# The last attention loop by blocks of queries with its own closing beside it, choice and gathering by image, and smaller groups of work in the fill

## The chip, the core and the metric

The kernel runs on one core of a Trainium2 chip. The core has a tensor engine (PE, with PEld for its loads of weights), a vector engine (DVE), a scalar engine (ACT), GpSimd (POOL) and SyncE (SP); each takes its instructions in order, and each of SP, ACT and POOL also issues DMAs from its own queue. The metric is the device time of one execution in microseconds, as the median of three runs.

## The reference, cut to what matters

There are two layers on x of four images, 4096 tokens (64 by 64) and 128 channels. Names are shortened here.

```python
# layer 0: three selective scans (forward, backward, sliced) over the tokens
xz = in_proj(groupnorm(x))                       # 256 channels u and 256 channels z, per token
for d in (forward, backward, sliced):            # d is an order of the tokens
    u = silu(causal_conv1d(u_d, conv_w, conv_b))           # 4 taps
    dt_raw, B, C = x_proj(u)                               # 8, 16 and 16 rows
    delta = softplus(dt_w @ dt_raw + dt_b)
    h[t] = h[t-1] * exp(delta[t] * A) + delta[t] * u[t] * B[t]   # 256 channels x 16 states
    y_d = (sum over states of h * C + D * u) * silu(z)
x = x + out_proj(y_f + y_b + y_s)

# layer 1, attention: 16 heads of width 8, q = k = v
t = layernorm(x)
q = ring_of_cosines(t + theta)
ctx = softmax(q q^T / sqrt(8)) q                 # 4096 x 4096 per head and image
x1 = layernorm(t + ctx @ w_comb.T + b_comb)
zf = cos(x1[:, :8]) * cos(ry)
t = x + layernorm(x1 + relu(zf @ w1.T + b1) @ w2.T + b2)

# layer 1, experts: 64 experts, each takes its 8 best tokens of an image
xn = layernorm(t)
probs = softmax(xn @ gate_w.T + gate_b, axis=tokens)
vals, idx = top_k(probs, 8)                      # per image and expert
pooled = sum over the 8 of xn[idx] * vals        # 64 x 128 per image
out = gelu(pooled @ weight1) @ weight2           # with bias rows
t = t + scatter_add(idx, out * vals)             # on the tokens that were chosen
```

All data are 32-bit floats.

## The kernel before, in words

**Order.** The program is recorded by hand: generators give one step at a `yield`, and a `Pace` turns credits into steps (`run(0.5)` gives half a step, so one step in two calls). Each engine then runs its instructions in the order in which they were recorded. `flow(pieces, width, apart)` runs up to `width` generators in turn, and starts the next one when the last one started has made `apart` steps. `Bank` hands out banks of PSUM; a piece that finds none yields and tries again.

**The fill** (up to about 2447 us). `Inputs` makes the inputs of the scans for all four images: per image `norm`, then for each of three orders four chunks of 1024 tokens (`of_chunk`), and beside the third order the four pieces of `gate`. A chunk is a convolution on PE (tile `cv`), Silu on ACT, projections on PE (`xd`, `dt`), a softplus in pieces (Abs and Relu, Exp, Ln and two Identity passes on ACT; three matmuls per half that sum them in tile `sp`, L415), an addition on DVE (L417), a product on DVE (L421) and stores to DRAM by POOL. Beside it `Scans.of_image(0)` runs the 384 scan steps of image 0. A step loads spread rows of delta and du, takes exp on ACT (L496), and has three instructions on DVE: product (L505), scan (L508), product (L510). Every four steps PE sums over the states in tile `y` (L516), and DVE adds D times u in tile `o` (L532), which POOL stores. The two are interleaved one step of scan to 0.98 steps of inputs. A matrix A for each order is loaded by 96 small DMAs on the ACT and POOL queues; `scan_weights` then takes its exp on ACT (L198) in the same place, before ACT copies the first normed tokens (L274).

**The opening and loops 0 to 2** (up to about 10453 us). After a short stage for the first `opening`, an attention `loop` runs per image, with the scans of the next image, the `opening` of the next and the closing (`after`) of the one before beside it. A loop has 1024 rounds: 4 groups of heads j, 8 blocks of 512 queries qb, 32 blocks of 128 keys kc, nested in this order. A round has eight passes for scores (L846), two exponentials of 128x1024 on ACT (L851, so 2048 per loop) and eight passes for sums over keys (L860). At the last kc, ACT copies the accumulator (tile `av`, L869), and POOL stores it: four DMAs to `d_ctx` (L875) and one to `d_sum` (L878).

**Closing.** `after(b)` inverts the sums of the softmax (`shares`: load of `sum`, L922, store of `d_share`), then for eight blocks of 512 tokens: `first` (loads of x, `cT` and `part`, product L937, `co` matmuls L944, normalization) and, after one cosine for all, `second` (`zt` L965, `h` L978, `fo` L988, two normalizations, `xT` L1009, `lg` L1017, stores to `d_t`, `d_xn` and `d_lg`). The loop has one bank of PSUM for all of it.

**Loop 3** (from about 10453 to 12813 us) has `after(2)`, `biases` and `gather(0)` beside it, at half a step per round. `gather(j)` takes two images at once: `choice` (Max8 over 4096 logits L1088, Exp with sums L1095, Max8 again L1101, match_replace L1105, a product L1107, a product with the share L1109) and eight `pool` calls (transposes `wt` L1124, matmuls `pool` L1133).

**The end** (12813 us on). `after(3)` in five parallel pieces with seven banks, `gather(1)`, then `answers`: 16 groups of four experts (`h` L1169, `hT`, Gelu L1187, `o` L1192), whose weights come as `w1` on the SP queue (1 MB per group) and four `w2` DMAs on the ACT queue (1 MB in all). Two groups of weights are recorded before the closing, three after `gather(1)`. At last `scatter` adds the answers to the tokens (L1253, L1260) and stores `out`.

Of the kernel before, what the change touches and what calls it, by code (L numbers as in the profile page):

```python
# [16 lines left out]
P = 128  # L17
C = 128
# [116 lines left out]
def scan_weights(nc, const, load, load_ps, ident, in_proj_w, out_proj_w, dirs):  # L135
# [55 lines left out]
    for i, (d, w) in enumerate(zip(dirs, ws)):  # L191
# [6 lines left out]
        nc.scalar.activation(w["A"], w["A"], AF.Exp)  # L198
        nc.vector.tensor_scalar_mul(w["A"], w["A"], -1.0)
# [3 lines left out]
class Inputs:  # L203
# [29 lines left out]
    def bank(self, name):  # L233
        while self.held == 3:
            yield
        self.held += 1
        return self.ps.tile([P, T], F32, tag="a", name=name)
# [17 lines left out]
    def norm(self, b):  # L255

        nc = self.nc
        while b - 1 in self.gated and self.gated[b - 1] < NC:
            yield
# [54 lines left out]
    def gate(self, b, g):  # L314
        nc, xn = self.nc, self.normed[b]
        s_g = self.piece.tile([P, 2, T], F32, tag="u", bufs=2, name=f"z_{b}_{g}")
        for m in range(2):
# [7 lines left out]
            yield  # L325
            nc.scalar.activation(s_g[:, m, :], ps, AF.Silu)
# [5 lines left out]
    def of_chunk(self, b, order, c):  # L332
        while b not in self.normed or (order == 2 and b not in self.sliced):
            yield
# [23 lines left out]
        for m in range(2):  # L358
            ps = yield from self.bank(f"cv_{key}_{m}")
            for g, cut in enumerate(halves):  # L360
                for k in range(4):
                    nc.tensor.matmul(  # L362
                        ps[:, cut], w["conv"][:, k, m * P : (m + 1) * P], reads(k, g), start=(k == 0), stop=(k == 3)
                    )
            banks.append(ps)
            yield
# [17 lines left out]
        while self.middle:  # L384
            yield
# [20 lines left out]
        nc.scalar.activation(ln, e, AF.Ln, bias=1.0)  # L406
# [3 lines left out]
        yield  # L410
        for m in range(2):
# [4 lines left out]
            yield  # L416
            nc.vector.tensor_add(r[:, m, :], r[:, m, :], ps)  # L417
# [9 lines left out]
class Scans:  # L427
# [23 lines left out]
    def of_image(self, b, made, queue=None):  # L451
# [18 lines left out]
        def load(s):  # L470
# [7 lines left out]
            for name, bufs in (("delta", 3), ("du", 4)):  # L478
                t = self.deep.tile([P, T], F32, tag=name, bufs=bufs, name=f"{name}_{b}_{s}")
                src = made[b, order, c][name][at : at + 16]  # L480
                by = queue if queue is not None and name == "du" else nc.sync
# [74 lines left out]
        for s in range(self.AHEAD):  # L556
            yield from have(s)
            load(s)
        exp(0)
# [8 lines left out]

        for s in range(n):
            if s + self.AHEAD < n:  # L570
                yield from have(s + self.AHEAD)
            late = s >= 4 and s % 4 in (1, 2)
            if late and s % 4 == 1:
# [9 lines left out]
            if late:  # L583
# [4 lines left out]
            if late and s % 4 == 2:  # L588
                out(s - 3, y)
                self.bank.leave()  # L590
            yield
            self.steps[b] += 1
        while not self.bank.free:
# [6 lines left out]
        out(n - 1, y)  # L600
        self.bank.leave()
# [3 lines left out]
class Attention:  # L605
# [3 lines left out]
    def __init__(self, tc, ctx, w, gate, cols, ident, bank, dram, t1, w_out, sums, sz, x):  # L609
# [63 lines left out]
        self.xn, self.logits, self.angled = {}, {}, {}  # L673
# [146 lines left out]
    def loop(self, b, beside):  # L820
# [3 lines left out]
        self.total[b] = self.dram.tile([H, L], F32, name=f"d_sum_{b}")  # L824
# [5 lines left out]
        rounds = [(j, qb, kc) for j in range(4) for qb in range(L // QB) for kc in range(NT)]  # L830
# [35 lines left out]
        def sums(j, qb, i):  # L866
# [5 lines left out]
            def store():  # L872
                for k in range(4):
# [5 lines left out]
                    out=self.total[b].rearrange("(k j) t -> j k t", j=4)[j, :, cut], in_=av[D::32, :]  # L879
                )  # L880

# [15 lines left out]
        for i in sorted(later):  # L897
            later[i]()

    def after(self, b):  # L900

        nc = self.nc
        tiles = self.t1[b].rearrange("(t p) c -> p t c", p=P)
        mid = self.dram.tile([P, NT, C], F32, name=f"d_x1_{b}")
        share = self.dram.tile([H, L], F32, name=f"d_share_{b}")
        self.t2[b] = self.dram.tile([P, NT, C], F32, name=f"d_t2_{b}")
        self.xn[b] = self.dram.tile([P, NT, C], F32, name=f"d_xn_{b}")
        if b // 2 not in self.logits:
            self.logits[b // 2] = self.dram.tile([2, E, L], F32, name=f"d_lg_{b // 2}")
        z = self.small.tile([P, NT, D], F32, tag="z", bufs=1, name=f"z_{b}")  # L910
# [7 lines left out]
        def shares():  # L918
            t = self.piece([P, 512], "p0", name=f"sum_{b}")
            nc.sync.dma_start(out=t, in_=self.total[b].rearrange("h (c t) -> (h c) t", t=512))  # L920
            yield
            nc.vector.reciprocal(t, t)  # L922
            nc.gpsimd.dma_start(out=share.rearrange("h (c t) -> (h c) t", t=512), in_=t)
            yield

        def first(g):
# [7 lines left out]
                out=part, in_=share[:, g * 512 : (g + 1) * 512].unsqueeze(1).to_broadcast([H, D, 512])  # L934
# [22 lines left out]
        def second(g):  # L957
# [14 lines left out]
            while self.hidden == self.n - 1:  # L972
                yield
            self.hidden += 1
            h = self.one.tile([P, 4, 512], F32, tag="h", bufs=self.n - 1, name=f"h_{b}_{g}")
# [46 lines left out]
            nc.gpsimd.dma_start(out=self.logits[b // 2][b % 2, :, g * 512 : (g + 1) * 512], in_=lg)  # L1022
# [394 lines left out]
```

## Time and profile before

| | us |
|---|---|
| median of 3 runs | 13271.63 (13271.44 to 13279.25) |
| the profiled execution, its time | 13276.74 |
| its span, first to last instruction | 13275.0 |
| last product of the fill's inputs (L421) starts | 2438.2 |
| first exponential of loop 3 | 10456.1 |
| last exponential of loop 3 | 12812.2 |
| busy over the span: PE, DVE, ACT, POOL | 12311.7, 8963.1, 10702.1, 3471.0 |

The page gives the busy time of every engine over the span, and the span in 40 equal slices of 332 us with a digit for each engine. Slices 1 to 8 are the fill, 9 to 31 the loops 0 to 2, 32 to 38 loop 3, and the last one and a half the end. A table of stretches gives the busy time of each engine in each stretch with the granted clock of PE and the DMA load. In groups by line, the last part of a row says how long the engine was idle ahead of these instructions, and what ended the idle time. The chain of waits follows the work that ended last back from the end.

### The profile page before, as it was taken

To read this page: it belongs to the slowest core of one execution; us is meant where nothing else is said; L and a number is where in the kernel's file an instruction comes from. 1 tells how busy PE (TensorE), PEld (TensorE's weight loads), DVE (VectorE), ACT (ScalarE), POOL (GpSimd) and SP (SyncE) were. 2 spreads that over 40 slices of the span, in tenths; PEclk is the share of its full clock that TensorE was granted. 3 is DMA by queue.
4 is the path that set the end of the run, shared out by engine and by line. 5 is a ranking of instruction groups with operands and counts; after the bars stand their busy time and mean duration, and the time that the engine had idled before them with its cause. 6 is when DMAs were issued, how large, how long until landed. Compare 5 with 4: busy or idle time off the path is not lost. (4 is left out here: it accounts for less than half of the span.)

```text
span 13275.0 us, 213812 instructions
## 1 busy us (share of the span) xinstructions
PE 12311.7 (93%) x85255; PEld 3959.8 (30%) x85255; DVE 8963.1 (68%) x8565; ACT 10702.1 (81%) x10807; POOL 3471.0 (26%) x4198
## 2 busy tenths in 40 slices
PE   7797879489999999999999999999999999999976
PEld 3333333222222222233332222333222222222224
DVE  6998989788888876988888778888874110000014
ACT  5665756289999998999999989999998888888851
POOL 2333334222333332333333223333331000000001
PEclk9888888699999999999999999999999999999986
DMA  5666666544444445544444454444443100000015
GB/s 143 185 185 176 190 175 195 172 127 118 121 121 117 115 119 136 130 109 117 114 106 114 116 140 126 110 114 114 112 107 96 43 16 9 9 18 21 12 36 180
DMA packets 686881, 1482.04 MB, mean 112 GB/s; under 512 B 184894, under 2 KB 301942, under 8 KB 685878
## 3 DMA queue, kind: packets, MB, share of 16 engines
q1 hardware_dynamic: 495182, 1049.44, 30.7%
q0 software_dynamic: 139584, 300.84, 7.3%
q10 hardware_dynamic: 51112, 118.08, 3.3%
q8 instruction: 667, 10.93, 0.3%
q14 instruction: 336, 2.75, 0.1%
HBM read 1158.83 MB, written 308.94 MB: 111 GB/s over the span
## 5 line engine op out<-in xcount | busy, mean ns | idle before, releaser
L851 ACT ACTIVATE e<-s 128x1024 f32<-128x1024 f32 x8192 | 7904.5, 1027 | 1015.6 <-PE s L846 788.9
L846 PE MATMUL s<-qm,qT 32*128 32x512 f32 x32768 | 5416.4, 642 | 109.4 <-DMA qT<-d_q 58.8
L860 PE MATMUL acc<-e,v 128*32 128x512 f32 x32768 | 4387.0, 607 | 23.0 <-ACT av L869 20.0
L509 POOL COPY ends<-h 128x1 f32<-128x1 f32 x1536 | 1835.7, 1195 | 4934.0 <-DVE h L508 4920.3
L846 PEld LDWEIGHTS s<-qm,qT 32*128 32x128 f32 x32768 | 1789.8, 184 | 3266.4 <-issue 1453.6
L860 PEld LDWEIGHTS acc<-e,v 128*32 128x32 f32 x32768 | 647.6, 108 | 3158.2 <-issue 3019.3
L508 DVE TENSOR_TENSOR_SCAN h<-dA,ends,dB 128x1024 f32<-128x1024 f32 x576 | 1374.4, 2386 | 186.1 <-ACT dA L496 128.0
L508 DVE TENSOR_TENSOR_SCAN h<-delta,ends,du 128x1024 f32<-128x1024 f32 x576 | 1354.1, 2351 | 160.0 <-ACT delta L496 88.5
L505 DVE TENSOR_TENSOR dB<-du,B 128x1024 f32<-128x1024 f32 x768 | 935.3, 1218 | 204.3 <-PE y L516 185.8
L496 ACT ACTIVATE dA<-delta,A 128x1024 f32<-128x1024 f32 x768 | 887.9, 1156 | 213.5 <-DMA delta<-d_delta 152.2
L496 ACT ACTIVATE delta<-delta,A 128x1024 f32<-128x1024 f32 x768 | 887.3, 1155 | 180.7 <-PE y L516 170.2
L510 DVE TENSOR_TENSOR du<-h,C 128x1024 f32<-128x1024 f32 x768 | 940.7, 1225 | 26.3
L510 DVE TENSOR_TENSOR dB<-h,C 128x1024 f32<-128x1024 f32 x768 | 940.7, 1225 | 26.3
L505 DVE TENSOR_TENSOR du<-du,B 128x1024 f32<-128x1024 f32 x768 | 933.9, 1216 | 0.0
L875 POOL DMA_DIRECT2D d_ctx<-av x512 | 262.6, 521 | 1646.4 <-ACT av L869 1642.8
L362 PE MATMUL cv<-xn,conv 128*128 128x512 f32 x1024 | 492.2, 640 | 40.6 <-DVE xn L299 26.5
L516 PE MATMUL y<-dB,sel 128*32 128x256 f32 x6144 | 496.0, 396 | 16.4 <-DVE o L532 16.4
L516 PE MATMUL y<-du,sel 128*32 128x256 f32 x6144 | 492.0, 393 | 6.1 <-DVE du L510 6.1
L508 DVE TENSOR_TENSOR_SCAN h<-dA,dB 128x1024 f32<-128x1024 f32 x192 | 446.9, 2328 | 56.8 <-ACT dA L496 35.4
L532 DVE SCALAR_TENSOR_TENSOR o<-us,D,y 128x256 f32<-128x256 f32 x384 | 206.2, 537 | 412.1 <-PE y L516 398.6
L508 DVE TENSOR_TENSOR_SCAN h<-delta,du 128x1024 f32<-128x1024 f32 x192 | 440.1, 2292 | 38.9 <-ACT delta L496 15.3
L415 PE MATMUL sp<-s,minus 128*128 128x512 f32 x384 | 223.1, 665 | 208.2 <-ACT s L409 208.2
(248 smaller groups left out, 7714.6 us busy)
## 6 DMA issues: line engine op xcount, KB each, us to landing
delta<-d_delta SPq DMA_DIRECT2D x768, 512.0 KB
du<-d_du SPq DMA_DIRECT2D x576, 512.0 KB
du<-d_du ACTq DMA_DIRECT2D x192, 512.0 KB
d_u<-u POOLq DMA_DIRECT2D x48, 1024.0 KB, 5.7
B<-d_bc SPq DMA_DIRECT2D x96, 512.0 KB
C<-d_bc SPq DMA_DIRECT2D x96, 512.0 KB
d_delta<-r POOLq DMA_DIRECT2D x48, 1024.0 KB, 5.4
d_du<-u POOLq DMA_DIRECT2D x48, 1024.0 KB, 6.7
```

The lines of the kernel that those rows point to most:

```text
L362: nc.tensor.matmul(ps[:, cut], w["conv"][:, k, m * P : (m + 1) * P], reads(k, g), start=(k == 0), stop=(k == 3))
L415: nc.tensor.matmul(ps[:, cut], sign, t[:, m, cut], start=(i == 0), stop=(i == 2))
L496: nc.scalar.activation(tiles["delta", s], t, AF.Exp, scale=A)
L505: nc.vector.tensor_mul(dB, du, spread[order, c, "B", j % 2])
L508: nc.vector.tensor_tensor_scan(h, dA, dB, first, ALU.mult, ALU.add)
L509: nc.gpsimd.tensor_copy(ends[order, c][:, at : at + 1], h[:, T - 1 :])
L510: nc.vector.tensor_mul(dB, h, spread[order, c, "C", j % 2])
L516: nc.tensor.matmul(y[32 * g : 32 * g + 32, : T // 4], self.sel[:, j // 2, :], hC[:, 256 * g : 256 * g + 256], start=(j == 0), stop=(j == 3),)
L846: nc.tensor.matmul(s_ps[:, k, :], qT[at : at + 32, kc * P : (kc + 1) * P], queries[j, qb][at : at + 32, :], start=True, stop=True,)
L851: nc.scalar.activation(e, s_ps, AF.Exp, scale=1.0 / math.sqrt(D))
L860: nc.tensor.matmul(accs[j, qb][32 * k : 32 * k + 32, :], v[:, kc, h * VW : h * VW + 32], es[i][k // 2][:, k % 2, :], start=(kc == 0), stop ...
L875: nc.gpsimd.dma_start(out=self.context[b][h * D : h * D + D, cut], in_=av[32 * k : 32 * k + D, :])
```

## The change

Five things are changed.

- **Fill.** A yield stands behind every half of a convolution and of a softplus sum; both additions L417 of a chunk come together, one step after the last matmul; Ln is recorded behind the two Identity passes. The two generators are interleaved 1 to 1.5, a second piece starts 10 steps behind the first in place of 6. The scans of image 0 have two banks in place of one, and `finish` (tile `o`) is recorded two scan steps later. The exp of A moves to just ahead of the first exp of the scans.
- **Loop 3 by blocks.** The last loop goes over qb outside and j inside, and `whole` tells when a block of queries has all its heads. `after` takes a range of blocks: 0 to 3 and 4 to 6 of image 3 are recorded beside loop 3, block 7 behind it. The share is 0.92 steps per round, and 1.5 once seven blocks are whole.
- **By image.** Logits are kept per image. `gather` takes images (0, 1), then 2, beside loop 3, and 3 at the end. `search` takes the eight best logits of seven blocks of image 3 ahead; the end looks at these 8 and the 512 of block 7.
- **Choice.** There is one Max8 in place of two (the eight values found go through Exp themselves), and no product with the share: it goes into a diagonal that replaces the identity in `wt` (now matmuls of 64 columns), and into `answers`.
- **End.** Four groups of weights are recorded right behind the loop and a fifth behind the closing; the closing has one piece in flight.

In the order of the changed program the closing of image 2 spans rounds 8 to 420 of loop 3, pool calls of images 0, 1 and 2 rounds 441 to 657, blocks 0 to 3 of image 3 rounds 667 to 870, blocks 4 to 6 rounds 903 to 995, and the search of image 3 follows at round 997. Between the fill and loop 3, the order on every engine is that of before.

```diff
@@ scan_weights
-        nc.scalar.activation(w["A"], w["A"], AF.Exp)
-        nc.vector.tensor_scalar_mul(w["A"], w["A"], -1.0)
@@ Inputs.of_chunk
                     nc.tensor.matmul(
                         ps[:, cut], w["conv"][:, k, m * P : (m + 1) * P], reads(k, g), start=(k == 0), stop=(k == 3)
                     )
+                yield
             banks.append(ps)
-            yield
+        yield
...
         nc.scalar.activation(e, e, AF.Exp, scale=-1.0)
-        nc.scalar.activation(ln, e, AF.Ln, bias=1.0)
         yield
         nc.scalar.activation(s, e, AF.Identity, bias=1.0)
         nc.scalar.activation(s, s, AF.Identity, bias=self.minus_one)
         yield
+        nc.scalar.activation(ln, e, AF.Ln, bias=1.0)
+        yield
+        banks = []
         for m in range(2):
             ps = yield from self.bank(f"sp_{key}_{m}")
             for cut in halves:
                 for i, (sign, t) in enumerate(((self.ident, e), (self.minus, s), (self.ident, ln))):
                     nc.tensor.matmul(ps[:, cut], sign, t[:, m, cut], start=(i == 0), stop=(i == 2))
-            yield
-            nc.vector.tensor_add(r[:, m, :], r[:, m, :], ps)
+                yield
+            banks.append(ps)
+        yield
+        for m in range(2):
+            nc.vector.tensor_add(r[:, m, :], r[:, m, :], banks[m])
             self.leave()
@@ Scans.of_image
+        if b == 0:
+            for w in self.ws:
+                nc.scalar.activation(w["A"], w["A"], AF.Exp)
+                nc.vector.tensor_scalar_mul(w["A"], w["A"], -1.0)
         exp(0)
...
+        def finish(s, y):
+            out(s, y)
+            self.bank.leave()
...
             step(s)
-            if late and s % 4 == 2:
-                out(s - 3, y)
-                self.bank.leave()
+            if turn == 2 and not alone:
+                finish(s - 3, y)
+            if turn == 0 and alone and s >= 8:
+                finish(s - 5, y)
@@ Attention.loop
+        turns = [(j, qb) for j in range(4) for qb in range(L // QB)]
+        if by_block:
+            turns.sort(key=lambda turn: turn[1])
+        rounds = [(j, qb, kc) for j, qb in turns for kc in range(NT)]
...
+                if by_block and j == 3:
+                    self.whole[b] = qb + 1
@@ Attention.after
-    def after(self, b):
+    def after(self, b, gs=range(L // QB)):
...
+        while self.whole[b] < blocks.stop:
+            yield WAIT
...
         yield from shares()
-        yield from flow((first(g) for g in range(NT // 4)), self.n, 8 // self.n)
+        yield from flow((first(g) for g in gs), self.n, 8 // self.n)
         yield from cosines()
-        yield from flow((second(g) for g in range(NT // 4)), self.n, 32 // self.n)
+        yield from flow((second(g) for g in gs), self.n, 32 // self.n)
@@ Experts: search is new, choice and pool by image
+        self.bring(images, prob, slice(0, blocks * QB))
+        yield
+        nc.vector.max(out=best[rows, :TOP], in_=prob[rows, : blocks * QB])
...
+            self.bring(images, prob, rest, rest.start)
+            self.bring(images, best, rest, TOP)
+            yield
+            nc.vector.max(out=top, in_=best[rows, : TOP + L - rest.start])
...
+        nc.scalar.activation(top, top, AF.Exp, bias=low)
...
-        nc.vector.max(out=top, in_=prob)
...
-        nc.vector.tensor_scalar_mul(w, w, share)
...
-            nc.tensor.transpose(ps[:, i * P : (i + 1) * P], self.chosen[j][:, at : at + P], self.ident)
+            nc.tensor.matmul(
+                ps[:, i * E : (i + 1) * E], self.chosen[b // 2][rows, at : at + P], self.diagonal[rows, b // 2, :],
+                start=True, stop=True,
+            )
@@ tile_kernel
-            first = Pace(scans.of_image(0, inputs.made, nc.scalar))
-            others = Pace(flow(inputs.pieces(range(nb)), 2, 6))
+            first = Pace(scans.of_image(0, inputs.made, True))
+            others = Pace(flow(inputs.pieces(range(nb)), 2, 10))
             while not first.done:
-                others.run(0.98)
+                others.run(1.5)
                 first.run(1.0)
...
-        last = Pace(last.parts, experts.biases(), *(experts.gather(j) for j in range(nb // 2 - 1)))
-        block.loop(nb - 1, lambda i: last.run(0.5))
+        last = Pace(
+            last.parts, experts.biases(),
+            *(part for images in pairs[:-1] for part in (experts.search(images, blocks), experts.gather(images))),
+            block.after(nb - 1, range(0, 4)), block.after(nb - 1, range(4, blocks - 1)),
+            experts.search(pairs[-1], blocks - 1),
+        )
+        block.loop(nb - 1, lambda i: last.run(0.92 if block.whole[nb - 1] < blocks - 1 else 1.5), True)
...
-            w = {g: experts.weights(stream, g) for g in range(2)}
+            experts.prefetch(end, 4)
             with ExitStack() as pieces:
-                block.pieces_of(pieces, 5, opening=False)
-                for _ in block.after(nb - 1):
+                block.pieces_of(pieces, 1, opening=False)
+                for _ in block.after(nb - 1, range(blocks - 1, blocks)):
                     pass
-            for _ in experts.gather(nb // 2 - 1):
+            experts.prefetch(end, 1)
+            for _ in experts.gather(pairs[-1], blocks - 1):
                 pass
```

## The prediction

> **What bounds the kernel now.** I read the page's slices first, for where each engine is full.
>
> ```profile
> PE   7797879489999999999999999999999999999976
> DVE  6998989788888876988888778888874110000014
> PEclk9888888699999999999999999999999999999986
> ```
>
> There are three regimes: the fill (slices 1 to 8) has DVE highest; the loops have PE full at full clock; the end (the last 1.4 slices) has nothing full and a low clock. The change touches the fill, loop 3 and the end, so each needs its own view.
>
> For the fill I asked for stretches (busy us and instructions of PE, PEld, DVE, ACT, POOL; then clock, DMA share, GB/s) and for DVE's groups between 149 and 2450 us.
>
> ```profile
> 149.00:500.00 351.00, 311.06 (x1036) 124.97 (x1036) 338.09 (x223) 254.39 (x203) 118.38 (x120) 0.91 0.64 189
> 500.00:750.00 250.00, 178.23 (x661) 72.83 (x664) 210.04 (x154) 130.43 (x109) 63.76 (x73) 0.79 0.60 172
> 750.00:1100.00 350.00, 318.90 (x1070) 127.55 (x1061) 336.56 (x224) 244.27 (x194) 127.20 (x140) 0.90 0.66 196
> 1100.00:1350.00 250.00, 177.09 (x643) 72.63 (x644) 206.51 (x152) 134.66 (x112) 76.28 (x103) 0.78 0.59 166
> ...
> L417 DVE TENSOR_TENSOR r<-r,sp 128x1024 f32<-128x1024 f32 x94 | 114.2, 1215 | 32.0 <-PE sp L415 31.9
> L532 DVE SCALAR_TENSOR_TENSOR o<-us,D,y 128x256 f32<-128x256 f32 x94 | 49.8, 530 | 57.8 <-PE y L516 57.8
> ```
>
> Per image there is a good stretch, in which DVE is 96% busy, and a bad one with 83 to 84%, in which PE and ACT are less busy too. So in the bad ones no engine is the limit: in-order queues wait for each other. The largest wait is DVE's for the sums y, recorded just ahead of `finish` and late behind convolutions on PE.
>
> For loop 3, the exponentials L851 per stretch, two to a round:
>
> ```profile
> 10456.00:10740.00 284.00, 245.55 (x254) 1.00 0.14 47
> 10740.00:12226.00 1486.00, 1244.41 (x1284) 1.00 0.04 11
> 12226.00:12376.00 150.00, 123.61 (x128) 1.00 0.11 38
> 12376.00:12606.00 230.00, 190.04 (x197) 1.00 0.05 14
> 12606.00:12812.00 206.00, 180.10 (x186) 1.00 0.01 2
> ```
>
> The last row has nothing beside it: 93 rounds, 2.215 us each. The others give 2.236, 2.314, 2.344 and 2.335 us: what stands beside the loop lengthens it, since PE is full.
>
> For the end, the chain of waits (start, length, what):
>
> ```profile
> 12820.23 2.50 DMA sum<-d_sum
> ...
> 13061.24 3.44 DMA prob<-d_lg
> 13064.81 4.44 DVE top L1088
> 13074.48 4.33 DVE topp L1101
> ...
> 13097.44 3.68 PE pool L1133 x16
> ```
>
> From 12813 to 13275 all 462 us are on the path: closing 248, choice 29, pools 43, answers and scatter 142.
>
> **Fill.** (a) Start. ACT's first copy of tokens waits until 46.95 us behind exp of A, whose DMAs stand on its own queue; the tokens' transposes ended at 40.3 us. Moved, it costs nothing more there and frees about 6 us. With 10 steps between pieces, chunk 0 passes PE ahead of most of chunk 1: two convolutions of chunk 1 (14.6 us by the timeline's 29.4 for four) leave its path, while the softplus then waits behind one `xd` and some convolutions that are new there (about 4 us). First product of the scans at 148 us before; I take 17 us earlier, of 10 to 25. (b) Bad stretches. At 96% of DVE, 500 to 750 would take 218 us in place of 250, 1100 to 1350 215, the third (217.7 busy of 260) 226, and 2310 to 2447 (113.8 of 137) 118: 120 us at most. `finish` two steps (some 10 us) later removes the 57.8 us before L532; the joined additions and finer groups remove some of the 32.0 before L417, and of the 37 us of waits for exp. (c) Against it: each next image's `norm` now has its six small DVE instructions with two trips over PE in one run, where scan steps stood between: about 5 us for each of three images, 15. I take 60% of 120, less 15, plus 17: 74, say 80; bounds 0 (waits only move) and 137. DVE's own work is unchanged to within a few us, so it sets the floor.
>
> **Opening and loops 0 to 2.** Nothing moves on any queue: 0.
>
> **Loop 3.** (a) Closing of image 3, blocks 0 to 6. From the rows: 0.099 us more on 642 rounds is 64 us for eight blocks of `second`, 8 us each, and 0.021 on 127 rounds 0.3 us a block for `first`. Seven blocks: 58 us. (b) Pools. (2.335 - 2.215) times 98.5 rounds is 12 us for 6 calls, 2 us per call with 20 passes on PE (4 transposes, 16 matmul passes). A call by image has 16 passes (8 of `wt` over 64 columns, 8 of `pool`), 1.6 to 2 us; 24 calls in place of 8: 38 to 48 less 16, so 27. (c) Choices: the row of 150 us has 8 us beyond 64 bare rounds, 4 of them pools; one more choice and one search, 5. Their DVE instructions (4.4 us each) hide behind PE unless an eviction is queued behind them; without that cover it is up to 4 us each. (d) Waits. `co` of image 2 is recorded at round 8 in place of 15, while its product had ended only 25 us after the first exponential (10481.4, timeline): 7 us of PE. Blocks 4 to 6 become whole at round 898 and are wanted at 903: storing, loading, inverting, storing and loading again took 17 us after the load of `sum` alone at the loop's start against 11.5 us here; 4 us. ACT's queue has exponentials behind exp(top), which waits for Max8 and a 2 MB load: 3 us. Sum 14. SP and POOL have slack: DMA share there is 0.01 to 0.19. Loop 3: +104; bounds 65 and 150.
>
> **End.** (a) The closing of block 7 alone. Here a rule speaks against the change. Rows: at the loop's start the load of `sum` was issued at 10464.44 behind 4.75 MB of loads on SP, and its product began at 10470.56, 6.1 us on; at the end, with an empty queue, 12820.23 and 12822.85, 2.6 us.
>
> ```profile
> 10464.44 0.32 SPq L920 DMA_DIRECT2D sum<-d_sum  x1
> 10470.56 3.35 DVE L922 RECIPROCAL sum<-sum 128x512 f32<-128x512 f32 x1 [15.82 <-DMA sum<-d_sum]
> ```
>
> The Trainium skill, "DMA: Bandwidth & Descriptors", Queues, rings and completion order, says that SP's and ACT's DMAs share the same 16 engines, each queue in its order. Now four groups of weights (8.4 MB) stand ahead of `sum` and `part`, and in the new program `part` is issued only when the last `w1` has landed. The fastest stretch of the end moved 377 GB/s: 22 us, say 25 with the start. By the rows alone I would have the product L937 at 20 us behind the loop as before; by the rule at 29. I take the rule, as the first row has its direction. From L937 on by the tail's timeline, one block alone: 9 us to `z`, then cosine 3, `zt` 2.5, `h` and relu 5, `fo` 4, two normalizations with sums 13, `xT` and `lg` 5, store 2: 43. So logits land at 72 us against 248. Slots of `h` and `fo` keep the cold rows (0.57 clock): a chain of one block fills PE less still. (b) Choice. The loads of 512 logits stand behind a fifth group and beside the first tokens for the scatter: 3 MB, 11 us for 3.5. Then Max8 over 520 (0.6, scaled from 4.4), exps 5.3, match_replace 4.5, product 4.4, small ones 1: 16, against 25.4. (c) Pools: a call took 5.3 us (passes of 0.22); now 8 + 8 passes, 3.5, and the eviction of half the size, 0.6: 4.1, eight calls 33 against 42.5. Pooling ends at 72 + 11 + 16 + 33 = 132 against 320. (d) Answers. Groups 2 to 4 of `w1` were issued only at 13122.9, behind waiting loads of x; now five groups are there, 23 MB remain: 61 us at 377 GB/s, where 13133 to 13220 took 87. I take 10 less: 132. The share on `answers` adds 0.5. End: 265 against 462, so -197; bounds -215 and -160 (weights at 250 GB/s, 10 us; no gain in the answers, 10; pools not cheaper, 10).
>
> **The sum** against the profiled execution's 13276.7 (span 13275.0): -80 + 104 - 197 = -173, 13103.7. The median of the runs lies 5.1 lower, so 13099, rounded to 13100. Time from 0.2% (27 us) on can be told from no change.
>
> **Rivals.**
> - The fill gains nothing: the waits before L532 reappear before L505 and L508, since the same PE queue stands behind (L505 already waits 8 us for y). For it: PE waits 203 us for ACT in L415, and Ln has only changed places. Against: the good stretches reach 96% with the same work. 13180.
> - The fill gains all: DVE at 96% throughout. Then 137 in place of 80: 13043.
> - Loop 3 and the weights at the dear ends (+150, -160): 13164.
> - Slower: the single bank in loop 3. Each use waits on PE for the eviction of the one before. There are 244 uses (15 blocks of 13, 24 pools of 2, one of bias) against 121, at 0.92 to 1.5 steps per round in place of 0.5, so as little as 1.5 us apart. Evictions take 0.3 to 0.7 us plus whatever DVE has queued. From 0.7 us of wait per use on, the whole gain is gone; at 1.5 us, 366 us more than my sum, 13466. Against it: PE's idle time before L846 in loop 3 was 3.8 us in all, and loops 0 to 2 carry over a step per round at 2550 to 2602 us. That the change does not do what it says I exclude: the recorded order has block 6 closed by round 995.
>
> **Numbers.** Forecast 0.59; nothing in the fill 0.17; everything in the fill 0.12; dear loop and weights 0.07; bank 0.05. Range 13020 to 13190: from half the way beyond the full fill, to the empty fill with some of the dear ends. Faster 0.94, within 0.2% 0.02, slower 0.04.
>
> **What would show it.** Right: the first exponential of loop 3 at 10376; loop 3 at 2460 us; 265 us behind it; no L532 wait over 10 us in sum; `part` landing about 28 us behind the loop. Wrong: bad stretches of DVE still at 84%; PE idle before L846 in tens of us in loop 3; rounds of 2.5 us near its end, which would mean the bank; `part` within 20 us, which would mean that the weights didn't hold it.

## The result and the profile after

The changed kernel takes 13122.04 us (median of 4 runs, 13120.72 to 13122.99) against 13273.36 us: a ratio of 0.9885, with a 95% interval of 0.9868 to 0.9902. The forecast was 13100. By the two profiled executions (spans 13275.0 and 13120.6 us):

| stage | before, us | after, us | change | forecast |
|---|---|---|---|---|
| start to the first exponential of loop 0 | 2706.0 | 2604.2 | -101.8 | -80 |
| loops 0 to 2, with what lies between, to the first exponential of loop 3 | 7750.1 | 7750.8 | +0.7 | 0 |
| loop 3, first exponential to the first of the last round | 2356.1 | 2471.9 | +115.7 | +104 |
| behind it, to the end of the span | 462.8 | 293.8 | -169.0 | -197 |

The page's slices (40 of 328 us; busy tenths, and the granted clock of PE) show where it went. In slices 1 to 8 PE has gone from sevens to eights in most places. The end, with a granted clock of 0.60 on average (0.61 before), takes 0.9 of a slice where it took 1.4.

```profile
PE   8898888399999999999999999999999999999995
...
PEclk8898888699999999999999999999999999999996
```

The first good and the first bad stretch of the fill, in the columns of before (busy us and instructions of PE, PEld, DVE, ACT, POOL; clock, DMA share, GB/s): the good one is as it was, and DVE is busy for 92% of the bad one, in place of 84%. The next pair reads the same.

```profile
149.00:500.00 351.00, 312.38 (x1048) 124.36 (x1048) 337.31 (x224) 232.36 (x186) 117.25 (x119) 0.89 0.64 190
500.00:750.00 250.00, 213.50 (x757) 86.83 (x757) 230.56 (x169) 160.42 (x132) 73.37 (x83) 0.85 0.64 189
```

DVE's groups in the fill (149 to 2450 us; after the bar: busy us, mean ns, idle time ahead of them). The additions L422 wait 6.4 us in place of 32.0, and `o`, L537, waits 0.6 us in place of 57.8.

```profile
L422 DVE TENSOR_TENSOR r<-r,sp 128x1024 f32<-128x1024 f32 x94 | 110.7, 1214 | 6.4 <-PE sp L417 6.4
...
L537 DVE SCALAR_TENSOR_TENSOR o<-us,D,y 128x256 f32<-128x256 f32 x96 | 51.0, 531 | 0.6 <-PE y L521 0.6
```

PE's groups in loop 3, 10354.93 to 12826.81 us. The last column, the idle time ahead of each group, is what to look at first: next to nothing waits (14.7 us in the rows of `s`, `acc` and `co` together, nothing in the rest), so the loop is as long as its passes.

```profile
L866 PE MATMUL s<-qm,qT 32*128 32x512 f32 x8184 | 1336.7, 641 | 5.8 <-ACT e L871 5.8
L880 PE MATMUL acc<-e,v 128*32 128x512 f32 x8180 | 1094.0, 607 | 5.3 <-ACT av L889 5.3
L1018 PE MATMUL fo<-w,h 128*128 128x128 f32 x480 | 69.5, 288 | 0.0
...
L974 PE MATMUL co<-w_comb,cT 128*128 128x128 f32 x120 | 21.9, 306 | 3.6 <-DVE cT L967 3.6
```

The end, from its chain of waits (start, length, what); the loop's last round began at 12826.8, and the times below are counted from there.

```profile
12848.17 6.08 DMA sum<-d_sum
...
12857.38 3.17 DMA part<-d_share
12860.67 0.70 DVE cT L967
...
12907.23 18.66 DMA best<-d_lg
12925.91 0.71 DVE top L1145
...
12941.10 1.98 PE wt L1181 x8
...
12976.61 1.97 PE h L1226 x8
```

The product L967 comes at 33.9 us, the logits have landed in DRAM at 79, Max8 starts at 99.1, the pool calls at 114.3, the answers at 149.8. Two places stand out: the load of `sum` is issued only at 21 us, and a load of 512 logits takes 18.7 us.

### The profile page after: what moved, and what is told of

The parts are those of the page before. It is cut to its first block, busy times and chain, and to the rows that moved or that the text cites. A ratio compares the mean times of both kernels' runs of the same rounds, so it can differ in the third digit from the quotient of the medians.

```text
span 13120.6 us, 214395 instructions
## 1 busy us (share of the span) xinstructions
PE 12316.4 (94%) x85447; PEld 3954.2 (30%) x85447; DVE 8997.7 (69%) x8649; ACT 10692.1 (81%) x10789; POOL 3486.8 (27%) x4200
## 5 line engine op out<-in xcount | busy, mean ns | idle before, releaser
L537 DVE SCALAR_TENSOR_TENSOR o<-us,D,y 128x256 f32<-128x256 f32 x384 | 205.9, 536 | 354.9 <-PE y L521 343.3
L550 POOL DMA_DIRECT2D d_y<-o x512 | 328.5, 669 | 276.3 <-DVE o L537 255.5
```

The source lines that it names most:

```text
L550: nc.gpsimd.dma_start(out=to.rearrange("p (i j) -> p i j", i=SLICES)[:, :, at : at + n], in_=rows.rearrange("p (i j) -> p i j", i=SLICES),)
```

## The experiments

Times are medians, ratios are to the kernel before, and the interval is in brackets. Beside the experiments the kernel before took 13275 to 13281 us.

**1. The fill alone.** The classes of the inputs and scans, the place of exp(A), the two banks and the interleaving of the changed kernel, put into the kernel before. Of its lines:

```diff
...
-            others = Pace(flow(inputs.pieces(range(nb)), 2, 6))
...
+            others = Pace(flow(inputs.pieces(range(nb)), 2, 10))
...
-                others.run(0.98)
+                others.run(1.5)
...
```

> The kernel before with the changed fill alone; loop 3 and the end are as before. In the changed kernel the first exponential of loop 0 came 101.8 us earlier (2604.2 for 2706.0), and loops 0 to 2 kept their lengths within 2 us. Theory: the stages are independent, so the whole of that stays: first exponential of loop 0 at 2604, loop 3 at 2356 us and 463 us behind it as before, total 13273 - 102 = 13171. Rival: part of what the fill saves is paid for later (the order of tiles and banks in the loops differs), then the total is above 13185.

Measured: 13161.4 us, 0.9915 [0.99, 0.993]. The first exponential of loop 0 is at 2602.1, loop 3 takes 2358.4 us as before. So the saving of the fill stays to the end of the program, and the stages add. The part behind loop 3 took 450.9 us, not 463: in the six profiled executions that have the old end it was 449 to 463 us, so about 10 us of the profile of before are scatter of that stage, and some 160 of the 169 us in the table above are the change's. Scatter of this size also separates the medians (116 us) from the 104 us by which loop 0 begins earlier.

**2. Tile `o` two steps later, alone.** My largest item for the fill, put into the kernel before.

```diff
-            if late and s % 4 == 2:
+            if late and s % 4 == 2 and queue is None:
                 out(s - 3, y)
                 self.bank.leave()
+            if s % 4 == 0 and s >= 8 and queue is not None:
+                out(s - 5, y)
+                self.bank.leave()
...
+        scans.bank = Bank(fill.enter_context(tc.tile_pool(name="s_bank", bufs=2, space=PSUM)), 2)
...
```

> The kernel before, with one edit of the fill: two banks for the scans of image 0, and tile o two scan steps later. In the kernel before, the vector engine waits 57.8 us ahead of o. Theory: a wait in front of an engine that is 96% busy in the good stretches is simply taken out, since there the engine has work queued behind it: 58 us less (50 to 60), 13215. Rival: in-order queues hold each other, so most of the wait comes back at the product or at the scan (waits for y and for exp), and the gain is under 20 us, above 13253.

Measured: 13273.7 us, 0.9997 [0.9989, 1.0006]: nothing. DVE's groups in its fill show why.

```profile
L508 DVE TENSOR_TENSOR_SCAN h<-dA,ends,dB 128x1024 f32<-128x1024 f32 x143 | 356.4, 2492 | 45.7 <-ACT dA L496 28.4 <-DVE dB L505 0.5
...
L505 DVE TENSOR_TENSOR dB<-du,B 128x1024 f32<-128x1024 f32 x190 | 231.4, 1218 | 23.5 <-PE y L516 23.5
...
L417 DVE TENSOR_TENSOR r<-r,sp 128x1024 f32<-128x1024 f32 x94 | 114.3, 1216 | 54.4 <-PE sp L415 54.2
...
L532 DVE SCALAR_TENSOR_TENSOR o<-us,D,y 128x256 f32<-128x256 f32 x94 | 49.6, 527 | 0.0
```

The 57.8 us ahead of `o` are gone, and are back at the instructions behind it: 15.5 us more ahead of the product (for the same `y`), 22 more ahead of the additions, 22 more ahead of the scans. DVE's idle time between the first scan and the last input was 197.7 us and is 200.1. That is what the rival said.

**3. The same edit undone in the changed kernel.**

```diff
-            if turn == 2 and not alone:
+            if turn == 2:
                 finish(s - 3, y)
-            if turn == 0 and alone and s >= 8:
-                finish(s - 5, y)
...
-        if alone:
-            finish(n - 5, y)
```

> The changed kernel with the one edit undone: tile o is recorded right behind the sums y again, two scan steps earlier; the second bank stays. If the later o is what emptied the wait (58 us before), the wait comes back in front of o and the total goes to 13122 + 58 = 13180 (13165 to 13185). If the finer pieces on PE had already made y early enough, the wait in front of o stays under 20 us and the total under 13142.

Measured: 13121.4 us, 0.9885 [0.9868, 0.9901], the changed kernel's time; by the traces the first exponential of loop 0 is 4.6 us later (2608.8). With `o` in its old place its wait is 19 us, not 58:

```profile
L537 DVE SCALAR_TENSOR_TENSOR o<-us,D,y 128x256 f32<-128x256 f32 x96 | 51.0, 531 | 19.1 <-PE y L521 19.0
```

So in the changed kernel `y` is nearly on time by itself. The wait ahead of `o` was a symptom; moving the one who waits neither cures it nor is needed.

**4. exp(A) moved, alone.**

```diff
-        nc.scalar.activation(w["A"], w["A"], AF.Exp)
-        nc.vector.tensor_scalar_mul(w["A"], w["A"], -1.0)
...
+        if b == 0:
+            for w in self.ws:
+                nc.scalar.activation(w["A"], w["A"], AF.Exp)
+                nc.vector.tensor_scalar_mul(w["A"], w["A"], -1.0)
         exp(0)
```

> The kernel before, with one edit of the fill: the exp of A moves to just ahead of the first exp of the scans. The whole fill brought the first product of the scans from 148.9 to 138.1 us for the scan (10.8 us earlier). Theory: 6 us of these are ACT's first copy of tokens, which no longer waits for the small loads of A: first scan at about 143, total 13267. Rival: the longer spacing of pieces makes the start (all 10.8 us or more come from it), and this edit gives nothing: 13273.

Measured: 13265.8 us, 0.9991 [0.9982, 1.0]. The fill shows none of it: the first scan starts at 147.1 (148.9 before, 147.3 in experiment 2, which doesn't have this edit), and loop 0 at 2706.4 (2706.0 before). The trace's shorter span comes from behind loop 3 (449.3 us), where this edit has nothing to change. ACT's timeline shows why the start stays:

```profile
28.79 15.93 ACTq L197 DMA_DIRECT2D A<-in_L_conv_A_log_s_dram  x16
...
46.12 2.84 ACT L272 COPY xn<-xt 128x1024 f32<-128x1024 f32 x3
```

With exp(A) out of the way, ACT's first copy of tokens still starts at 46.12 us, where it started at 46.95. ACT itself issues the last 16 small loads of A, until 44.72 us, and the copy stands behind that in ACT's order. The edit moved the exp and left the loads where they were.

**5. Halves of convolutions and sums, alone; and whole groups in the changed kernel.** As neither `o` nor exp(A) carried the fill, I tried the size of the groups both ways. The rate keeps the last chunk at its place among the scan steps.

```diff
                     nc.tensor.matmul(
                         ps[:, cut], w["conv"][:, k, m * P : (m + 1) * P], reads(k, g), start=(k == 0), stop=(k == 3)
                     )
+                yield
             banks.append(ps)
-            yield
+        yield
...
-            yield
+                yield
...
-                others.run(0.98)
+                others.run(1.297)
```

> The kernel before, with one edit of the fill: a yield behind every half of a convolution and of a softplus sum (one step more behind the last convolution), and 1.297 steps in place of 0.98 per scan step, so that the last chunk keeps its place among the scan steps. The additions, Ln, tile o, the exp of A and the spacing stay as before. The later tile o alone gave nothing, and taking it away from the changed kernel lost nothing, so one of the other edits empties the bad stretches. Theory (grain): PE's queue is stopped by whole groups of 16 convolutions and of 12 sums, and halves are enough: PE's wait for ACT ahead of the sums sp falls from 203 us to under 100, the total to 13277 - 70 = 13207 (13190 to 13220). Rival (distance): what counts is how many steps lie between Ln and the sums that read it, and between the last sum and the addition; then halves alone leave 150 us or more of that wait and give under 25 us: 13252 or more.

The counterpart takes these yields out of the changed kernel, at a rate of 1.079:

> The changed kernel with one edit undone: a convolution and a softplus sum are whole groups again (no yield behind a half, nor the step behind them), at 1.079 steps in place of 1.5 per scan step, so that the last chunk keeps its place. Ln behind the Identity passes, one step ahead of the sums, the joined additions, tile o two steps later and the spacing stay. Theory (grain): most of the 90 us of the fill goes back: 13122 + 70 = 13192 (13170 to 13205). Rival (distance): the gain stays, 13122 to 13145.

Measured: halves alone 13295.1 us, 1.0011 [1.0004, 1.0017], a little slower; whole groups in the changed kernel 13438.7 us, 1.0117 [1.0101, 1.0132], 317 us behind the changed kernel. Both miss both expectations, and they have a flaw: the number of steps in a chunk had changed, and the spacing between two chunks, counted in steps, had not. In the second one a chunk starts 10 of 13 steps behind the one before, so that the two should hardly overlap; DVE's additions waited 313 us in its fill, where the changed kernel's waited 6. Experiment 6 tests whether the spacing did that.

**6. The same two with the spacing mended.**

```diff
-            others = Pace(flow(inputs.pieces(range(nb)), 2, 6))
+            others = Pace(flow(inputs.pieces(range(nb)), 2, 9))
```

(9 of 17 steps in the first, with 1.255 steps per scan step; 7 of 13 in place of 10, with 1.059, in the second.)

> As fine (halves of convolutions and sums in the kernel before), with the second piece started 9 steps behind the first in place of 6, and 1.255 steps per scan step. A chunk has 12 steps in the kernel before, 17 in fine and 19 in the changed kernel, so 6 and 10 put two chunks half a chunk apart there, while fine stood at a third of a chunk and coarse at three quarters (where the next convolution is recorded behind the sums of the chunk before). If that distance between chunks was what spoiled fine, the halves now give 13207 (13190 to 13225). If halves are of no use without Ln's place, the joined additions and the later tile o, the total stays at 13265 or more.

> As coarse (whole groups in the changed kernel), with 7 of its 13 steps between pieces in place of 10, and 1.059 steps per scan step, so that two chunks stand half a chunk apart again. If the 317 us that coarse lost came from its chunks no longer overlapping, and whole groups cost little by themselves, the total comes back to 13122 to 13150. If whole groups are what makes the bad stretches bad, the fill is that of the kernel before again: 13122 + 90 = 13212 (13190 to 13225). If the addition one step behind the sums is too near them, it is later still: above 13250.

Measured: halves alone 13283.2 us, 1.0005 [0.9996, 1.0013]: still nothing. Whole groups in the changed kernel 13152.6 us, 0.9906 [0.9891, 0.992]: 30 us behind the changed kernel, and 3 us beyond the first expectation's range. So the spacing (with the rate that belongs to it) was worth 286 of the 317 us. By the first scan and the first exponential of loop 0:

| fill | halves | the other edits | first scan, us | loop 0, us | between |
|---|---|---|---|---|---|
| before | no | no | 148.9 | 2706.0 | 2557 |
| halves alone, spacing 6 of 17 | yes | no | 148.3 | 2726.8 | 2578 |
| halves alone, spacing 9 of 17 | yes | no | 133.3 | 2711.1 | 2578 |
| changed, whole groups, 10 of 13 | no | yes | 136.4 | 2921.9 | 2786 |
| changed, whole groups, 7 of 13 | no | yes | 134.1 | 2634.8 | 2501 |
| changed | yes | yes | 138.1 | 2604.2 | 2466 |

So the halves are worth 31 us once the rest is there. Without it they cost some 20 us behind the first scan, which the earlier start hides at 9 of 17. The other 71 us belong to what is left: about 15 to the start, and 56 to Ln behind the two Identity passes with a step between it and the sums, the joined additions, the extra step in `gate`, and waiting steps that no longer count for the spacing. Which of these was not tried apart.

The traces show two waits that shrink. The first is PE's for ACT ahead of the sums `sp` between 149 and 2340 us (line waited for: us, times, longest): before, then halves alone at 9 of 17.

```profile
PE sp L415 <- ACT s L409: 184.5, 24, 10.0
```

```profile
PE sp L416 <- ACT s L410: 142.2, 26, 10.7
```

And the changed kernel with whole groups at 7 of 13, then the changed kernel itself:

```profile
PE sp L416 <- ACT ln L409: 46.2, 17, 3.1
```

```profile
PE sp L417 <- ACT ln L410: 45.4, 17, 3.1
```

With a step between the Identity passes and the sums, PE no longer stands for up to 10.7 us for ACT with the scan's `y` and the next convolutions queued behind it: with the smaller rows, its waits for ACT there are 198 and 147 us in these two long fills, and 64 and 78 us in the two short ones. But the longer of the short fills has the smaller wait, so this is not where the halves gain. The second is DVE's wait ahead of the additions, in the same four fills and the same order:

```profile
DVE r L417 <- PE sp L415: 25.3, 13, 6.5
```

```profile
DVE r L418 <- PE sp L416: 72.4, 38, 5.2
```

```profile
DVE r L420 <- PE sp L416: 56.0, 15, 8.6
```

```profile
DVE r L422 <- PE sp L417: 5.9, 5, 1.5
```

Halves alone take DVE's wait ahead of `o` from 54.4 to 20.0 us, and the additions wait 47 us more: the wait moves once more. With the other edits the wait ahead of `o` is under 1 us. The two together are 80, 92, 57 and 7 us, which ranks the four fills as the last column of the table does. Ln's place with the step behind it, and the joined additions one step behind the sums, are both candidates for the 56 us; that either is the cause is argued, not shown.

The pair with 6 and 9 of 17 also settles the start: the first scan is at 148.3 in the one and 133.3 in the other, and the spacing is the only edit between them, apart from the rate.

**7. Denser work beside loop 3.** The rival of the single bank.

```diff
-        block.loop(nb - 1, lambda i: last.run(0.92 if block.whole[nb - 1] < blocks - 1 else 1.5), True)
+        block.loop(nb - 1, lambda i: last.run(1.5), True)
```

> The changed kernel with 1.5 steps per round beside the whole of loop 3, in place of 0.92 until seven blocks are whole. No instruction is added or left out. In the changed kernel the loop's 2471.9 us are 2457.6 us of PE's own busy time and 14.7 us of gaps. Theory (PE's sum): the work beside the loop costs its passes on PE wherever it stands, so the loop stays at 2472 us within 8 and the total at 13122 within 10. Rival (the single bank of PSUM): with uses of the bank 1.5 us apart, PE waits for evictions; 0.7 us or more per use on some 170 uses of it adds 100 us or more, 13220.

Measured: 13142.1 us, 0.9901 [0.9886, 0.9916]; loop 3 takes 2492.5 us, 20.6 more than in the profile after (in the six other executions with the loop of the changed kernel it took 2465.7 to 2472.0). PE's waits in loop 3 (line waited for: us, times, longest):

```profile
PE co L974 <- DVE cT L967: 10.6, 1, 10.6
PE s L866 <- ACT e L871: 7.7, 6, 1.9
PE acc L880 <- ACT av L889: 5.3, 20, 0.3
PE wt L1181 <- DVE chosen L1169: 4.4, 2, 2.4
PE xT L1039 <- DVE x1r L780: 0.3, 1, 0.3
```

No row has PE wait for the bank to be emptied: the copies of `h`, `fo`, `wT` and `pooled` do not appear. What grew is the wait for data where a chain of loads and DVE work had not come through yet, 7.0 us at the first `co` and 4.4 us behind the choices; these and smaller gaps make 13.5 us, and the score passes took 5 us more. Both expectations miss: no wait for the bank shows at this density, and density is not free either.

**8. The order of loads at the end.** The last block's loads (with the inversion and the product L967 that hang on them) are recorded ahead of four groups of weights; the last logits ahead of the fifth; both. The edit of both:

```diff
-            experts.prefetch(end, 4)
+            early = end.enter_context(tc.tile_pool(name="e_stream0", bufs=4))
             with ExitStack() as pieces:
                 block.pieces_of(pieces, 1, opening=False)
-                for _ in block.after(nb - 1, range(blocks - 1, blocks)):
+                closing = block.after(nb - 1, range(blocks - 1, blocks))
+                for _ in range(4):
+                    next(closing)
+                for g in range(4):
+                    experts.ahead.append((experts.weights(early, g), early))
+                for _ in closing:
                     pass
+            gathering = experts.gather(pairs[-1], blocks - 1)
+            next(gathering)
             experts.prefetch(end, 1)
-            for _ in experts.gather(pairs[-1], blocks - 1):
+            for _ in gathering:
                 pass
```

> The changed kernel; in the end the loads of sum, x, cT and part of the last block are recorded ahead of the four groups of weights on the SP queue (the w2 loads keep their place on the ACT queue). In the changed kernel the product of cT and part starts 33.9 us behind the last exponential. Theory: 14 us of these are queueing behind the weights, and a single chain of small loads without them takes about 20: product at 20 us, everything behind it 12 to 14 us earlier, total 13109. Rival: the w2 loads on the other queue use the same DMA engines and hold it as much, or the weights come late for the answers instead: product above 30 us or the gain given back in the answers, total 13118 or more.

Measured: 13110.1 us, 0.9875 [0.986, 0.989]. The product L967 starts at 24.2 us behind the loop in place of 33.9, and the stage is 11.5 us shorter (282.3).

> The changed kernel; in the end the two loads of the last 512 logits are recorded ahead of the fifth group of w1 on the SP queue. In the changed kernel they are issued at once with that group and with 11 loads of t from POOL, and take 18.7 us to land, where a lone load took 3.4 us. Theory: SP's queue order is most of it; landing in 6 to 9 us, total 13122 - 11 = 13111. Rival: the t loads on POOL's queue and the w2 loads on ACT's (together 4 MB) share the DMA engines and hold the logits just the same: landing 15 us or more, total 13119 or more.

Measured: 13112.6 us, 0.9877 [0.9862, 0.9892]. The logits take 8.7 us in place of 18.7, and the stage is 12.4 us shorter (281.4).

> The changed kernel with both orders of the end: the last block's loads ahead of the first four groups of weights, and the last logits ahead of the fifth. If both waits are on the one chain that sets the end, and the answers do not lack weights for it, the two gains add: 13122 - 13 - 11 = 13098. If the answers are set by the weights' arrival, the gain is under 10 us: 13112 or more.

Measured: 13098.3 us (13090.0 to 13102.8), 0.9866 [0.985, 0.9883], the fastest version here; the stage takes 269.7 us, 24.1 less, so the two add. Its chain of waits, with the loop's last round at 12826.0:

```profile
12837.01 4.06 DMA sum<-d_sum
...
12844.36 3.94 DMA part<-d_share
...
12894.38 8.11 DMA best<-d_lg
```

Nothing was given back in the answers: these last 142.5 us, against 144.0. In this order the weights come no later for the answers, and the small loads come sooner.

## Why the prediction was right or wrong

**The total** is right to 22 us because three misses partly cancel: the fill gave 22 more than forecast, loop 3 cost 12 more and the end gave 28 less. That closeness is in part luck.

**Fill, size nearly right, reason wrong.** The step that failed is that recording `finish` two steps later would take out the 57.8 us before L532 and shorten the fill by them. It does take them out there (0.6 us remain), but experiments 2 and 3 show that this edit is worth nothing in either kernel. The first rival had the mechanism, for this edit: the waits reappear before L505 and L508 (and before L417), since the same PE queue stands behind. It was wrong that the fill therefore gains nothing. What emptied the bad stretches lies in the other edits, 31 us of it in the halves once the others are there (experiment 6); which of the others stays open. One candidate is the row that I had, PE's wait of 203 us for ACT in L415, and passed over with "Ln has only changed places"; the joined additions, which I named beside it, are another. In the start the size was right and the reason half wrong: the first scan is 10.8 us earlier in the profile after and 15.6 to 16.6 in five other executions with this fill, for 17 forecast. But exp(A), which was to free 6 of them, gives none that can be seen, since ACT's issuing of the loads of A holds the first copy just as long (experiment 4), and the spacing of the chunks gives 15 (experiment 6), where I had 14.6 less 4. `norm` in one run costs 5.3 us of DVE's waits in three images, for the 15 that I had put down.

**Opening and loops 0 to 2** came out at 0.7 us, as forecast.

**Loop 3, mechanism right, one term too small.** If each of PE's passes is counted from the end of the one before it, the loop's 2471.9 us are 2457.6 us of passes and 14.7 us of gaps (before: 2346.4 and 10.0; each pair exceeds the length by under half a us, since the last pass crosses the end). Of the growth, closing passes are 78.3 us, pool passes 29.6, the loop's own 3.2, gaps 4.6. The pools were forecast at 27. The closing was forecast at 58 for seven blocks, and 11.4 us a block were measured, for my 8.3 (before: 11.7, counted in the same way). The mis-sized step is the bare round of 2.215 us: the stretch that I read it from still held 16 pool passes (1.9 us), so that the round is 2.19, and each of 642 rounds of closing had some 0.025 us more in it than I counted; with the 127 rounds of `first` that brings 8.3 to 10.7 us a block, and the rest to 11.4 stays open. The choices and waits, forecast at 19, are the remaining 8. The bank was rightly given little. None of the rows with idle time is a wait for it.

**End, 28.8 us longer than forecast.** Step by step:

| step | forecast, us | measured, us |
|---|---|---|
| product L967 behind the loop | 29 | 33.9 |
| product to logits landed | 43 | 45.3 |
| logits landed to Max8 | 11 | 19.9 |
| choice | 16 | 15.2 |
| eight pool calls | 33 | 35.5 |
| answers and scatter | 132 | 144.0 |

The rule that I had set against the change (the Trainium skill, "DMA: Bandwidth & Descriptors", Queues, rings and completion order: both queues' DMAs share the same engines, each queue in its order) took the right side of the trace's rows: 33.9 us, where the rows alone gave 20. Experiment 8 takes the order out, and 9.7 us go. (The row at 10470.56 that I took for a product is the inversion L922; the time read from it stands.) I applied the same rule too weakly one stage later: 3 MB were counted ahead of the last logits, and they shared the engines with about 5 MB, the fifth group and 11 loads of `t` from POOL; 18.7 us, of which 10 are the SP queue's order. The largest miss is the answers, where 10 us were to be saved by having five groups of weights at hand. They took 144.0 us, for 141.5 before (144.1 in experiment 1, which has the old end). The kernel before was hardly worse off there, since the groups issued at 13122.9 had 10 us to the first `h`; and the other 11 can only come as slots are freed. From 12977 to 13047 us the DMA engines were busy for 88% of the time at 319 GB/s. This fits that the loads of these 11 groups set the stage in both kernels; no run here takes them away. My 377 GB/s was the fastest stretch, not this one.

**One sum of the rivals does not come out.** The forecast for the fill with the dear ends of loop 3 and of the weights is 13276.7 - 80 + 150 - 160 = 13187, or 13182 for the median, not 13164; and the three items behind the -160 are 30 us in all, which gives -167. Neither bears on the forecast.

## What to carry to other kernels

A wait can belong to the queue that is late, and not to the instruction that shows it: before an instruction is moved out of its wait, ask who else waits for that queue, for they may show the same wait next, as they did here. When the grain of interleaved work is changed, everything counted in its steps (spacing, rate) has to be rescaled, or the experiment measures the phase and not the grain (286 of 317 us here). Behind a loop, record the small loads that a serial chain hangs on ahead of the bulk that only has to be there later: two such swaps were worth 24 us here.

## What the runs showed of the hardware that was not expected

- The last load of logits took 3.4 us in the kernel before. In the changed kernel a load of 512 logits per expert took 18.7 us with 1 MB of `w1` ahead of it on its own queue and loads of `t` and `w2` on the others, and 8.1 to 8.7 us with only the others' loads beside it.
- ACT's own issuing of 16 small loads of A lasted from 28.8 to 44.7 us (experiment 4), and its first copy of tokens began at 46.1; taking three exps out of its way moved that copy by 0.8 us, which is within its scatter (45.9 to 47.0 in four executions without that edit).
- PE had 14.7 us of gaps in the 2472 us of loop 3, so work recorded beside it cost what its passes take: 11.4 us for the closing of a block, 2.1 us for a pool call.
- The old end varied from 449 to 463 us between executions; with the changed end and its order of loads as it is, it was 292 to 294 us in five profiled executions.
